# Projecting B with time on partitions, multiplying it by x four states at a time, and moving the clip and the last products to GpSimd

## The chip, the cores and the metric

The kernel runs on one core of a Trainium2 chip. The core has five engines that each work through their own list of instructions in order: TensorE (PE: matrix products; PEld is its weight load), VectorE (DVE), ScalarE (ACT), GpSimd (POOL) and SyncE (SP, which here only starts transfers). They wait for each other through semaphores alone. The metric is device time in microseconds; the median of several runs is compared.

## The reference

The input is 32 sequences ("batches") of 512 time steps and 256 channels. Each goes through three residual layers: a gated feed-forward layer, a state-space layer, and the first feed-forward layer again.

```python
def reference(x, ...):
    x = x + 0.5 * ffn(_layernorm(x), w_gate, w_up, w_down)
    x = x + ssm(_layernorm(x), W_in, b_in, W_dt1, b_dt1, W_dt2, b_dt2, A, D)
    x = x + 0.5 * ffn(_layernorm(x), w_gate, w_up, w_down)
    return x

def ffn(x, w_gate, w_up, w_down):          # 704 inner columns
    # fp4_linear: both operands are rounded to a grid of 8 magnitudes, in blocks of 16 with a
    # scale of max|x| / 6 each, and then multiplied
    h = silu(fp4_linear(x, w_gate)) * fp4_linear(x, w_up)
    return fp4_linear(h, w_down)

def ssm(x, W_in, b_in, W_dt1, b_dt1, W_dt2, b_dt2, A, D):   # 16 states, rank 64
    BC = x @ W_in + b_in
    Bm, Cm = BC[..., :16], BC[..., 16:]
    dt = clip(softplus((x @ W_dt1 + b_dt1) @ W_dt2 + b_dt2), 1e-07, 1e6)
    A_bar = exp(A * dt)
    B_barX = expm1(A * dt) / (A * dt) * dt * Bm * x
    # along time: h[t] = A_bar[t] * h[t-1] + B_barX[t], for each of 256 channels x 16 states
    return sum(h * Cm, axis=state) + D * x
```

## The kernel before

The weights are rounded to the grid once and stay in SBUF. Then each batch passes through `ffn 0`, `ssm` and `ffn 1`, and several batches are in work at a time.

**Order.** No loop decides which instruction stands where. Each operation is first recorded (`op`, L307 on) with its engine, a name and the tiles that it reads and writes. `Plan.run` then writes them out by a heap: of all operations whose inputs are written and whose buffers are free, the one with the smallest place comes next. The place is a number from the table `WHEN` (L31), by the operation's name and its count, plus `PERIOD` times the batch (L327). So every engine's list is fixed when the program is built, the same places hold for each batch, and the middle of the program repeats itself batch after batch. Lists are worked through strictly in order: an instruction that waits holds up everything behind it on its engine.

**The feed-forward layer.** `layernorm` (L507 to L522) takes statistics on DVE, four tiny operations on POOL, and writes the normalized rows on ACT. `quantize` rounds a tile to the grid: `top` (largest magnitude of each block, L544), `scale` (L546), `rinv` (L548) and `quotient` (L550) on DVE, `square` (L554) and `curve` (L556) on ACT, `grid` on PE (L563), `rounded` on ACT (L569) and `value`, times the scale, on POOL (L570). It works in the PSUM tile `q`, of which there is one, so roundings follow one another. A batch has four tiles of 128 time steps. Each tile takes `gate` and `up` (PE, L676) in two halves of 352 columns, `silu` (ACT, L686), the product of the two, a rounding of 704 columns, a turn (PE L710, ACT L715) and `down` (PE L722, L726, ACT L729). The product is made on POOL (`product`, L699), after ACT has copied `up` out of PSUM (`up copy`, L696). For the pair named in `BY_DVE`, tile 0 of `ffn 0`, DVE makes it from PSUM instead (`up silu`, L692, twice).

**The state-space layer.** Channels lie on partitions, in two halves `c` of 128, and time along the row. `bc` (L741) projects x to 32 rows, 16 of B and 16 of C. ACT adds their bias (L745), and one transfer puts them in DRAM as `rows` (L748). `dt1` (L741, bias L752) and `dt2` (L757) lead to `softplus` (ACT, L761, in PSUM) and to the clip `dt` on DVE (L764). Then, for each half and each two states (`NG` = 2):

- `load b` (L780) and `load c` (L782) fetch two rows of B and of C into all 128 partitions, 512 KB each;
- `exp` (L789) and `tanh` (L792) on ACT, of which the second writes one of two PSUM tiles `eb`;
- `x b` on POOL (L796): B times x, for both states in one instruction;
- `e` (L803), `e x b` (L806) and `scan` (L809) on DVE, for each state;
- `h c` on POOL (L812), and `sum states` on PE (L818).

In `x b` time is the outer and the state the inner loop. x is repeated over the two states; B's tile and the output are stepped through 512 numbers apart:

```python
bx().rearrange("p n l -> p l n"),
xT()[:, c, :].unsqueeze(2).to_broadcast([P, L, NG]),
bn().rearrange("p n l -> p l n"), ALU.mult),
```

All loads of B and C stand in SP's one list. Each waits until POOL has let go of the buffer that it fills; there are two buffers of each kind.

Of the kernel before, what the change touches and what calls it, by code (L numbers as in the profile page):

```python
# [16 lines left out]
P = 128  # L17
# [14 lines left out]
        "weights load": (7249, 7248, 7249, 7249, 6726, 6726, 6642, 6642, 6642, 6841, 6841, 6841,  # L32
        6841),
        "weights x top": (7249, 7065, 7353),
        "weights x scale": (7250, 7248, 7385),
        "weights x rinv": (7250, 7248, 7391),
        "weights x quotient": (7250, 7248, 7391),
        "weights x square": (7250, 7249, 7392),
        "weights x curve": (7250, 7249, 7392),
        "weights x grid": (7250, 7249, 7557),  # L40
        "weights x rounded": (7250, 7249, 7557),
        "weights x value": (7250, 7249, 7558),
        "weights turn": (7251, 7251, 7249, 7249, 7558, 7558),
        "weights turned": (7251, 7251, 7250, 7251, 7558, 7558),
        "weights load down": (7065, 6579),
        "weights h top": (7558, 6642),
        "weights h scale": (7571, 6642),
        "weights h rinv": (7571, 6642),
        "weights h quotient": (7571, 6643),
        "weights h square": (7590, 6643),  # L50
        "weights h curve": (7590, 6643),
        "weights h grid": (7590, 6643),
        "weights h rounded": (7590, 6643),
        "weights h value": (7795, 7065),
        "weights turn down": (7795, 7795, 7699, 7661),
        "weights turned down": (7897, 7814, 8179, 7699),
        "weights zero rows": (8077, 8345),
        "in load": (0,),
        "ffn 0 stats": (1267, 1773, 601, 2361),
        "ffn 0 mean": (1913, 2355, 1536, 3584),  # L60
        "ffn 0 var + eps": (4038,),
        "ffn 0 rstd": (4045,),
        "ffn 0 - mean": (3609,),
        "ffn 0 shift": (4249,),
        "ffn 0 normal": (4499, 5056, 6579, 4467),
        "ffn 0 x top": (6643,),
        "ffn 0 x scale": (6726,),
        "ffn 0 x rinv": (6822,),
        "ffn 0 x quotient": (6835,),
        "ffn 0 x square": (6841,),  # L70
        "ffn 0 x curve": (6873,),
        "ffn 0 x grid": (6880,),
        "ffn 0 x rounded": (6950,),
        "ffn 0 x value": (6969,),
        "ffn 0 xqT turn": (7065, 7129),
        "ffn 0 xqT turned": (7136, 7168),
        "ffn 0 tile 0 gate": (7353, 7251),
        "ffn 0 tile 0 silu": (7437, 7321),
        "ffn 0 tile 0 up": (7577, 7558),
        "ffn 0 tile 0 up silu": (7584, 7571),  # L80
        "ffn 0 tile 0 h top": (7590,),
        "ffn 0 tile 0 h scale": (7609,),
        "ffn 0 tile 0 h rinv": (7661,),
        "ffn 0 tile 0 h quotient": (7705,),
        "ffn 0 tile 0 h square": (7737,),
        "ffn 0 tile 0 h curve": (7808,),
        "ffn 0 tile 0 h grid": (7814,),
        "ffn 0 tile 0 h rounded": (7897,),
        "ffn 0 tile 0 h value": (8045,),
        "ffn 0 tile 0 turn h": (8301, 8192),  # L90
        "ffn 0 tile 0 turned h": (8352, 8339),
        "ffn 0 tile 0 down": (8397,),
        "ffn 0 tile 0 sum": (8461,),
        "ffn 0 tile 1 gate": (7385, 7392),
        "ffn 0 tile 1 silu": (7449, 7507),
        "ffn 0 tile 1 up": (7622, 7667),
        "ffn 0 tile 1 up copy": (7718, 7699),
        "ffn 0 tile 1 product": (7795,),
        "ffn 0 tile 1 h top": (7923,),
        "ffn 0 tile 1 h scale": (8000,),  # L100
        "ffn 0 tile 1 h rinv": (8032,),
        "ffn 0 tile 1 h quotient": (8121,),
        "ffn 0 tile 1 h square": (8179,),
        "ffn 0 tile 1 h curve": (8205,),
        "ffn 0 tile 1 h grid": (8217,),
        "ffn 0 tile 1 h rounded": (8275,),
        "ffn 0 tile 1 h value": (8416,),
        "ffn 0 tile 1 turn h": (8493, 8441),
        "ffn 0 tile 1 turned h": (8544, 8512),
        "ffn 0 tile 1 down": (8563,),  # L110
        "ffn 0 tile 1 sum": (8781,),
        "ffn 0 tile 2 gate": (8083, 8064),
        "ffn 0 tile 2 silu": (8096, 8070),
        "ffn 0 tile 2 up": (8134, 8345),
        "ffn 0 tile 2 up copy": (8256, 8390),
        "ffn 0 tile 2 product": (8429,),
        "ffn 0 tile 2 h top": (8576,),
        "ffn 0 tile 2 h scale": (8653,),
        "ffn 0 tile 2 h rinv": (8704,),
        "ffn 0 tile 2 h quotient": (8729,),  # L120
        "ffn 0 tile 2 h square": (8813,),
        "ffn 0 tile 2 h curve": (8838,),
        "ffn 0 tile 2 h grid": (8857,),
        "ffn 0 tile 2 h rounded": (8953,),
        "ffn 0 tile 2 h value": (8979,),
        "ffn 0 tile 2 turn h": (9088, 9081),
        "ffn 0 tile 2 turned h": (9165, 9126),
        "ffn 0 tile 2 down": (9222,),
        "ffn 0 tile 2 sum": (9267,),
        "ffn 0 tile 3 gate": (8077, 8109),  # L130
        "ffn 0 tile 3 silu": (8089, 8211),
        "ffn 0 tile 3 up": (8928, 8985),
        "ffn 0 tile 3 up copy": (9069, 9094),
        "ffn 0 tile 3 product": (9101,),
        "ffn 0 tile 3 h top": (9357,),
        "ffn 0 tile 3 h scale": (9376,),
        "ffn 0 tile 3 h rinv": (9440,),
        "ffn 0 tile 3 h quotient": (9472,),
        "ffn 0 tile 3 h square": (9510,),
        "ffn 0 tile 3 h curve": (9529,),  # L140
        "ffn 0 tile 3 h grid": (9587,),
        "ffn 0 tile 3 h rounded": (9613,),
        "ffn 0 tile 3 h value": (9677,),
        "ffn 0 tile 3 turn h": (9837, 9843),
        "ffn 0 tile 3 turned h": (9869, 9856),
        "ffn 0 tile 3 down": (9920,),
        "ffn 0 tile 3 sum": (9984,),
        "ssm stats": (8768, 8992, 9517, 10048),
        "ssm mean": (9325, 9369, 9933, 10093),
        "ssm var + eps": (10099,),  # L150
        "ssm rstd": (10150,),
        "ssm - mean": (10157,),
        "ssm shift": (10163,),
        "ssm normal": (10182, 10169, 10227, 10176),
        "ssm xT turn": (10233, 10246),
        "ssm xT turned": (10304, 10310),
        "ssm bc": (10425,),
        "ssm bc bias": (10489,),
        "ssm rows": (10656,),
        "ssm dt1": (10317,),  # L160
        "ssm dt1 bias": (10451,),
# [120 lines left out]
        "ffn 1 tile 3 sum": (18157,),  # L282
        "out store": (19712,),
}


class Buf:

# [598 lines left out]
```

## Time and profile before

| What | Value |
|---|---|
| Median of 3 runs | 3603.8 us (3603.49 to 3605.61) |
| The profiled execution's own time | 3604.13 us |
| Its span, first to last instruction | 3602.2 us |
| Mean granted TensorE clock | 0.984 |
| Busy over the span: DVE, ACT, PE, POOL | 3409.9, 3385.7, 3348.0, 3332.3 us |
| Results stored, first to last | 395.7 to 3598.4 us |
| Transfers moved | 578.36 MB, 161 GB/s |

All figures but the median are of one execution, taken by the hardware profiler. A line such as `L764` is line 764 of the kernel. A group of instructions is shown as `out<-in`, partitions x elements, and `xcount | busy us, mean ns of one | idle time of the engine just before them <-what ended it`. Instructions that follow each other on an engine overlap a little, so the mean duration times the count is more than the busy time. What an instruction takes of its engine's list is better read from the timeline, from one start to the next start.

### The profile page before, as it was taken

To read this page: it belongs to the slowest core of one execution; us is meant where nothing else is said; L and a number is where in the kernel's file an instruction comes from. 1 tells how busy PE (TensorE), PEld (TensorE's weight loads), DVE (VectorE), ACT (ScalarE), POOL (GpSimd) and SP (SyncE) were. 2 spreads that over 40 slices of the span, in tenths; PEclk is the share of its full clock that TensorE was granted. 3 is DMA by queue.
4 is the path that set the end of the run, shared out by engine and by line. 5 is a ranking of instruction groups with operands and counts; after the bars stand their busy time and mean duration, and the time that the engine had idled before them with its cause. 6 is when DMAs were issued, how large, how long until landed. Compare 5 with 4: busy or idle time off the path is not lost. (4 is left out here: it accounts for less than half of the span.)

```text
span 3602.2 us, 51333 instructions
## 1 busy us (share of the span) xinstructions
PE 3348.0 (93%) x16604; PEld 2443.6 (68%) x16826; DVE 3409.9 (95%) x5280; ACT 3385.7 (94%) x5813; POOL 3332.3 (93%) x1963
## 2 busy tenths in 40 slices
PE   5779999999999999999999999999999999999966
PEld 3457777667767767777766776776777776777654
DVE  3699999999999999999999999999999999999992
ACT  4689999999999999999999999999999999999973
POOL 2589999999999999999999999999999999999992
PEclk9899999999999999999999999999999999999988
DMA  1354545444545545454544454444555454445440
GB/s 45 112 173 166 173 164 176 165 169 165 176 171 170 165 158 175 170 173 164 177 165 169 165 176 170 170 165 159 176 171 173 163 177 165 168 161 169 171 170 12
DMA packets 186652, 578.36 MB, mean 161 GB/s; under 512 B 19664, under 2 KB 54032, under 8 KB 186384
## 3 DMA queue, kind: packets, MB, share of 16 engines
q1 hardware_dynamic: 184816, 574.89, 46.7%
q8 instruction: 133, 2.18, 0.2%
q14 instruction: 135, 1.11, 0.1%
q10 hardware_dynamic: 1568, 0.18, 0.0%
HBM read 556.12 MB, written 18.87 MB: 160 GB/s over the span
## 5 line engine op out<-in xcount | busy, mean ns | idle before, releaser
L676 PE MATMUL pt<-w_guT,xqT 128*128 128x352 f32 x4096 | 1317.4, 466 | 26.1 <-DVE dt L764 16.3
L812 POOL TENSOR_TENSOR hs<-hs,bc 128x1024 f32<-128x1024 f32 x512 | 1214.0, 2371 | 9.3 <-DVE hs L809 2.6
L809 DVE TENSOR_TENSOR_SCAN hs<-ab,eb 128x512 f32<-128x512 f32 x1024 | 1202.4, 1197 | 4.5
L796 POOL TENSOR_TENSOR bx<-xT,bc 128x1024 f32<-128x1024 f32 x512 | 1171.2, 2294 | 30.3 <-DVE eb L806 15.9
L676 PEld LDWEIGHTS pt<-w_guT,xqT 128*128 128x128 f32 x4096 | 753.3, 192 | 409.7 <-DVE dt L764 24.0
L792 ACT ACTIVATE eb<-dt,a_half 128x512 f32<-128x512 f32 x1024 | 708.1, 700 | 36.1 <-DVE hs L809 29.5
L806 DVE SCALAR_TENSOR_TENSOR eb<-eb,a_inv,bx 128x512 f32<-128x512 f32 x1024 | 734.9, 743 | 2.7
L722 PE MATMUL pt<-w_dT,hqT 128*128 128x256 f32 x3072 | 717.0, 383 | 14.8 <-ACT hqT L715 14.8
L789 ACT ACTIVATE ab<-dt,a_sb 128x512 f32<-128x512 f32 x1024 | 700.8, 727 | 1.5
L803 DVE SCALAR_TENSOR_TENSOR eb<-ab,eb 128x512 f32<-128x512 f32 x1024 | 684.5, 682 | 11.4 <-ACT eb L792 7.6
L722 PEld LDWEIGHTS pt<-w_dT,hqT 128*128 128x128 f32 x3072 | 580.1, 192 | 140.4 <-ACT hqT L715 32.9
L818 PE MATMUL py<-ident,hs 128*128 128x128 f32 x4096 | 536.1, 276 | 26.1 <-POOL hs L812 25.8
L818 PEld LDWEIGHTS py<-ident,hs 128*128 128x128 f32 x4096 | 469.4, 142 | 102.0 <-POOL hs L812 38.3
L570 POOL TENSOR_TENSOR h_q<-h_q,h_sc 128x704 f32<-128x704 f32 x258 | 360.3, 1397 | 53.2 <-ACT h_q L569 52.6
L699 POOL TENSOR_TENSOR h<-h,sl 128x704 f32<-128x704 f32 x224 | 379.0, 1692 | 27.4 <-ACT h L696 22.4
L544 DVE TENSOR_REDUCE q<-h 128x44 f32<-128x704 f32 x258 | 227.0, 880 | 68.6 <-POOL h L699 43.8
L710 PE MATMUL pt<-ident,h_q 128*128 128x128 f32 x1536 | 237.0, 278 | 41.2 <-ACT h L696 24.1
L563 PE MATMUL q<-h_m,eye 128*128 128x192 bf16 (+1 forms) x873 | 191.6, 305 | 70.9 <-ACT h_m L556 62.0
L710 PEld LDWEIGHTS pt<-ident,h_q 128*128 128x128 f32 x1536 | 180.5, 141 | 110.3 <-ACT h L696 51.8
L563 PEld LDWEIGHTS <-eye 128*128 128x128 bf16 x1300 | 125.2, 99 | 183.9 <-issue 106.8
L715 ACT COPY hqT<-pt 128x256 f32<-128x256 f32 (+1 forms) x512 | 233.9, 487 | 6.1 <-PE pt L710 5.7
L686 ACT ACTIVATE sl<-pt 128x352 f32<-128x352 f32 x512 | 222.5, 463 | 16.6 <-PE pt L676 13.8
(78 smaller groups left out, 4134.6 us busy)
## 6 DMA issues: line engine op xcount, KB each, us to landing
bc<-rows SPq DMA_DIRECT2D x1024, 512.0 KB, 4.1
x<-in_L_attn_x_dram SPq DMA_DIRECT2D x32, 512.0 KB, 5.2
out_dram<-x SPq DMA_DIRECT2D x32, 512.0 KB, 7.3
rows<-bc SPq DMA_DIRECT2D x32, 64.0 KB, 3.4
xn<-in_L_ffn_w_up_dram SPq DMA_DIRECT2D x6, 128.0 KB, 2.2
h<-in_L_ffn_w_down_dram SPq DMA_DIRECT2D x2, 352.0 KB, 3.4
xn<-in_L_ffn_w_gate_dram SPq DMA_DIRECT2D x5, 128.0 KB, 2.2
w_dt_sb<-in_L_attn_W_dt_dram ACTq DMA_DIRECT2D x2, 64.0 KB, 5.5
```

Source lines behind the costliest of these rows:

```text
L676: pe.matmul(to()[:, :HALF], lhsT=xqT()[:, c, j * P : (j + 1) * P], rhs=w_guT()[:, c, o : o + HALF], start=(c == 0), stop=(c == NC - 1),)
L699: op("POOL", "product", lambda sl=sl, h=h: g.tensor_tensor(h(), h(), sl(), ALU.mult), [h, sl], [h])
L710: pe.transpose(pt()[:, i * P : (i + 1) * P], hq()[:, kcol[k] : kcol[k] + P], ident)
L722: pe.matmul(po()[:, :DM], lhsT=hqT()[:, k, :], rhs=w_dT()[:, k, :], start=(k == 0), stop=False,)
L789: op("ACT", "exp", lambda c=c, i=i, k=k, ab=ab: s.activation(ab()[:, i, :], dt()[:, c, :], AF.Exp, scale=a_sb[:, c, k : k + 1]), [(dt, c)] ...
L792: op("ACT", "tanh", lambda c=c, i=i, k=k, eb=eb: s.activation(eb[i](), dt()[:, c, :], AF.Tanh, scale=a_half[:, c, k : k + 1]), [(dt, c)], ...
L796: op("POOL", "x b", lambda c=c, bx=bx, bn=bn: g.tensor_tensor(bx().rearrange("p n l -> p l n"), xT()[:, c, :].unsqueeze(2).to_broadcast([P ...
L803: op("DVE", "e", lambda i=i, ab=ab, eb=eb: v.scalar_tensor_tensor(eb[i](), ab()[:, i, :], 1.0, eb[i](), ALU.add, ALU.mult), [(ab, i), eb[i ...
L806: op("DVE", "e x b", lambda c=c, i=i, k=n + i, eb=eb, bx=bx: v.scalar_tensor_tensor(eb[i](), eb[i](), a_inv[:, c, k : k + 1], bx()[:, i, : ...
L809: op("DVE", "scan", lambda i=i, h=h, ab=ab, eb=eb: v.tensor_tensor_scan(h()[:, i, :], ab()[:, i, :], eb[i](), 0.0, ALU.mult, ALU.add), [(a ...
L812: op("POOL", "h c", lambda h=h, cn=cn: g.tensor_tensor(flat(h()), flat(h()), flat(cn()), ALU.mult), [h, cn], [h])
L818: pe.matmul(py()[:, j, :], lhsT=h()[:, i, j * P : (j + 1) * P], rhs=ident, is_transpose=True, start=False, stop=False, skip_group_check=True,)
```

## The change

- **B.** It is projected by itself, with time on partitions: for each 128 time steps, 16 columns and a product with a row of ones for the bias (`project b`). ACT copies the result out as `bT`, 128 x 64. Four transfers write it to DRAM as `rows_b`, where the four states of a group (`XG` = 4) lie side by side for each time step.
- **`load b`** fetches one group of four states, 1 MB, into all partitions. `x b` works on four states and half of the time steps, 128 x 256 x 4 = 1024 numbers per partition as before. B's tile is now read in the order in which it lies; x is repeated over four states; the output is still stepped through 512 numbers apart. There are as many `x b` as before.
- **C and dt.** C's 16 rows and `dt1`'s 64 rows come from one product of 80 rows (`project`, `project bias`).
- **The clip** `dt` moves from DVE to POOL; `softplus` now writes SBUF.
- **Products.** All tiles' products are made on POOL, with `up copy` on ACT.
- **Places.** New numbers for all operations; batches 0, 1, 30 and 31 have tables of their own, and the weights use batch 0's.

```diff
+FIRST = {
...
+PRODUCT_BY_DVE = set()
+VALUE_BY_DVE = set()
+CLIP_BY = "POOL"
...
-        o.at = (WHEN[o.name][k] + self.batch * PERIOD, len(self.ops))
+        table = self.tables.get(self.batch, WHEN)
+        o.at = (table[o.name][k] + self.batch * PERIOD, len(self.ops))
...
-    BY_DVE = {(0, 0)}
...
-    plan = Plan()
+    plan = Plan({0: FIRST, 1: SECOND, NB - 2: LAST_BUT_ONE, NB - 1: LAST})
...
-        op("PE", "bc", lambda: project(pbc()[: 2 * N, :], w_in_sb), [xT], [pbc])
-        bc = new(sp, [2 * N, L], F32, "bc", 1)
...
+        def project_b():
+            for j in range(NJ):
+                to = pb()[:, j * N : (j + 1) * N]
+                for c in range(NC):
+                    pe.matmul(to, lhsT=xT()[:, c, j * P : (j + 1) * P], rhs=w_b_sb[:, c, :],
+                              start=(c == 0), stop=False)
+                pe.matmul(to, lhsT=one_row, rhs=b_b_sb, start=False, stop=True)
+
+        op("PE", "project b", project_b, [xT], [pb])
+        bT = new(sp, [P, NJ, N], F32, "bT", 2)
+        op("ACT", "b turned", lambda: s.copy(flat(bT()), pb()[:, : NJ * N]), [pb], [bT])
+        rows_b = new(dr, [N // XG, L, XG], F32, "rows_b", 2)
...
+                for i in range(N // XG):
+                    nc.sync.dma_start(
+                        rows_b()[i].rearrange("(j p) n -> p j n", p=P),
+                        bT()[:, :, i * XG : (i + 1) * XG])
...
-            op("DVE", "dt", lambda c=c: v.tensor_scalar(
-                dt()[:, c, :], p2[c](), 1e-7, 1e6, ALU.max, ALU.min), [p2[c]], [(dt, c)])
...
+                op("POOL", "dt", lambda c=c: g.tensor_scalar(
+                    dt()[:, c, :], dt()[:, c, :], 1e6, 1e-7, ALU.min, ALU.max),
+                   [(dt, c)], [(dt, c)])
...
+                if n % XG == 0:
+                    bn = new(st, [P, L, XG], F32, "bn", 2)
+                    bx = new(st, [P, XG, L], F32, "bx", 2)
+                    op("SP", "load b", lambda n=n, bn=bn: nc.sync.dma_start(
+                        bn(), rows_b()[n // XG].partition_broadcast(P)), [rows_b], [bn])
+                    for o in range(0, L, L * NG // XG):
+                        t = slice(o, o + L * NG // XG)
+                        op("POOL", "x b", lambda c=c, bx=bx, bn=bn, t=t: g.tensor_tensor(
+                            bx()[:, :, t].rearrange("p n l -> p l n"),
+                            xT()[:, c, t].unsqueeze(2).to_broadcast([P, L * NG // XG, XG]),
+                            bn()[:, t, :], ALU.mult), [(xT, c), bn], [(bx, o)])
```

## The prediction

> **What bounds the kernel now.** I read the totals by engine first, then busy time by stretches of the span.
>
> ```profile
> PE 3348.0 (93%) x16604; PEld 2443.6 (68%) x16826; DVE 3409.9 (95%) x5280; ACT 3385.7 (94%) x5813; POOL 3332.3 (93%) x1963
> ```
> ```profile
> 0.00:135.60 135.60, 83.88 (x291) 50.46 (x294) 45.18 (x100) 67.36 (x106) 34.25 (x38) 0.92 0.18 56
> 1600.00:2000.00 400.00, 385.72 (x1940) 283.54 (x1967) 397.76 (x619) 395.02 (x680) 390.25 (x229) 1.00 0.50 170
> 3517.60:3602.20 84.60, 55.91 (x217) 38.91 (x217) 14.81 (x28) 30.82 (x55) 19.07 (x15) 0.84 0.04 13
> ```
> The columns after the length are PE, PEld, DVE, ACT and POOL busy. In the middle four engines are almost full: DVE 99.4%, ACT 98.8%, POOL 97.6%, PE 96.4%. DVE sets the pace, and no other engine is far behind it. Before the first scan (135.6 us) and after the last (3517.6 us) all stand idle most of the time.
>
> The timeline of the stores gives the beat: one batch per 1779.05 - 1672.60 = 106.4 us.
>
> ```profile
> 1672.60 0.43 SPq L849 DMA_DIRECT2D out_dram<-x  x1
> 1779.05 0.43 SPq L849 DMA_DIRECT2D out_dram<-x  x1
> ```
> So the execution's 3604.1 us (3602.2 of span and 1.9 around it, 0.3 above the median of the runs) is 32 x 106.4 = 3405 and 199 for both ends. Per batch DVE is busy 0.994 x 106.4 = 105.8 us, ACT about 105.0 (394.5 of 400 in most stretches), POOL 103.7 (389.9 of 400). The change touches the beat and the ends; I work out both.
>
> **The beat, on DVE.** The groups that are removed, kept or moved:
>
> ```profile
> L764 DVE TENSOR_SCALAR dt<-pt 128x512 f32<-128x512 f32 x64 | 40.4, 671 | 14.9 <-ACT pt L761 14.9
> L692 DVE TENSOR_TENSOR h<-pt,sl 128x352 f32<-128x352 f32 x64 | 32.8, 512 | 13.3 <-PE pt L676 10.2
> L796 POOL TENSOR_TENSOR bx<-xT,bc 128x1024 f32<-128x1024 f32 x512 | 1171.2, 2294 | 30.3 <-DVE eb L806 15.9 <-DMA bc<-rows 14.2
> L812 POOL TENSOR_TENSOR hs<-hs,bc 128x1024 f32<-128x1024 f32 x512 | 1214.0, 2371 | 9.3 <-DVE hs L809 2.6 <-DMA bc<-rows 1.5 <-PE pt L676 1.2
> L570 POOL TENSOR_TENSOR x_q<-x_q,x_sc 128x1024 f32<-128x1024 f32 x67 | 129.7, 1936 | 60.5 <-ACT x_q L569 60.5
> L699 POOL TENSOR_TENSOR h<-h,sl 128x704 f32<-128x704 f32 x224 | 379.0, 1692 | 27.4 <-ACT h L696 22.4 <-issue 2.7 <-DVE h_sc L546 1.6
> ```
> In the timeline two clips take 0.58 + 0.60 us of DVE's list, from start to start, and the two `up silu` 0.61 + 0.63. Per batch 2.4 us go.
>
> Something comes back, and only the new program's order shows it. In one batch of the repeating part, 17 DVE instructions read what the instruction just ahead wrote; before there were 4. New are 6 `e` to `e x b`, 3 `top` to `scale`, 3 `scale` to `rinv` and 2 `e x b` to `scan`; 1 went with `up silu`. The trace prices this:
>
> ```profile
> 1639.92 1.41 DVE L806 SCALAR_TENSOR_TENSOR eb<-eb,a_inv,bx 128x512 f32<-128x512 f32 x2
> 1641.24 1.21 DVE L809 TENSOR_TENSOR_SCAN hs<-ab,eb 128x512 f32<-128x512 f32 x1
> 1700.78 0.76 DVE L806 SCALAR_TENSOR_TENSOR eb<-eb,a_inv,bx 128x512 f32<-128x512 f32 x1
> 1701.64 1.22 DVE L809 TENSOR_TENSOR_SCAN hs<-ab,eb 128x512 f32<-128x512 f32 x1
> ```
> In the first pair of lines two `e x b` take 1.32 us, 0.66 each, and the scan reads the earlier one. In the second the scan reads the one right ahead and starts 0.86 us after it: 0.20 more. `scale` to `rinv` is 0.22 us when adjacent and 0.11 otherwise. No row has `e` to `e x b` or `top` to `scale` adjacent; 0.11 and 0.20 bound them, and I take 0.18, nearer the row with the same shape. 9 x 0.18 + 3 x 0.11 + 2 x 0.20 = 2.35, at least 1.7. So DVE changes by -0.7 to +0.1 us per batch; I take -0.2, a beat of 106.2.
>
> The Trainium skill, "VectorE: DVE Perf Modes", section "The DRAIN you can't avoid", says that a Vector instruction waits for an empty pipe in any case and that waits between chained ones cost nothing extra. The trace differs (0.86 against 0.66). By the page DVE would save the whole 2.4 us and ACT would set a beat of about 105.8.
>
> **The beat, on ACT.** Two more `up copy` at 0.33 us start to start, a 64-column copy at about 0.15 (256 columns take 0.26, 512 take 0.47), one bias less at 0.57, and 6 `square` to `curve` adjacent where 2 were, 0.15 each (0.79 against 0.64): 0.67 + 0.15 - 0.57 + 0.60 = +0.85. Table loads stay at 9 per batch. ACT comes to 105.8, just under DVE.
>
> **The beat, on POOL.** It gains a product (1.64 us start to start) and two clips. No row shows a one-input POOL operation of 512 numbers. Memsets give a lower bound: 204 ns for 128 columns and 98 for one, so 0.52 us for 512; the 16-fold `value` row scaled to 512 gives 1.06. I take 0.8, or 1.6 per batch. What `x b` costs now is the open price. Its old form (x repeated twice, B strided) takes 2.24 us from start to start; the flat product `h c` 2.33; `value`, whose scale is repeated 16 times, 1.89 for the same 1024 numbers. A repeated operand is cheaper, so a fourfold repeat and B in order should lie between 1.89 and 2.24; I take 2.05, and 2.33 as the upper end should the step of the output cost more. Without `x b` POOL is 103.7 - 16 x 2.24 + 1.64 + 1.6 = 71.1, with 2.05 it is 103.9; between the ends, with the clips' bounds, 100.8 to 108.9. Behind a clip that waits for `softplus` stand POOL's products and `h c`, hence DVE; the 2.3 us that POOL has free per batch cover that.
>
> The skill's "GPSIMD Engine Reference", section 4.1, speaks against the move as such: elementwise work belongs on VectorE, GpSimd being about twice as slow. The rows agree (704 numbers take 1692 ns as POOL's product and 879 as DVE's `quotient`), which matters only if POOL becomes the bound. Section 7 charges about one cycle per number for reading in steps over 8 bytes. The old `x b` reads B that way and is still quicker than the flat `h c`; by the rule the change would save 0.85 us on each `x b` (an estimate at that page's 1.2 GHz).
>
> PE loses a 512-column projection (4 rows of 0.6 us) and gains 12 matmuls of 16 columns (24 rows, at 0.11 us by the shortest weight load in the trace): about even, and 3.8 us are free per batch. Transfers: the four `rows b` write 2048 pieces of 16 bytes per batch. In the trace's packet records a 64-byte packet took 11 ns and a 4-byte one 9, so this adds some 20 us of packet time over 16 engines, 1.3 us per batch, to DMA engines half idle. If it were not hidden, it would come to 40 us in all. `load b` moves the same bytes in half as many transfers. On SP `load c` stands behind it as before; a load of 512 KB landed in 4.1 us, so 1 MB should in some 8, and each buffer now lasts two `x b`, about 13 us.
>
> **The ends.** At the start, roundings follow one another in the single `q`.
>
> ```profile
> 46.22 1.23 DVE L544 TENSOR_REDUCE pt<-xn 128x64 f32<-128x1024 f32 x1 [10.26 <-ACT w_guT L624]
> 62.72 0.90 DVE L544 TENSOR_REDUCE q<-h 128x44 f32<-128x704 f32 x1 [0.85 <-ACT h_q L569]
> 91.48 0.89 DVE L544 TENSOR_REDUCE q<-h 128x44 f32<-128x704 f32 x1 [5.87 <-POOL h L699]
> ```
> The third weight block waited 10.3 us, and tile 3's rounding began at 91.5, four after tile 0's with gaps of 6.6 to 13. In the new order the weight blocks run on, and tile 0, the second `down` block and tiles 1 to 3 follow directly, their gates and products ahead. With x quotients 6.4 apart (18.67, 25.04), the third at 34.7 as before, and five roundings 6.6 apart from about 47, tile 3's begins at 73: 18 us earlier. PE's gates and the new queue ahead of `exp` (two `x b` stand before the clips on POOL) may cost some of it: I take 14, between 0 and 20.
>
> At the tail the last scan is followed by one `ffn 1`:
>
> ```profile
> 3553.63 0.90 DVE L544 TENSOR_REDUCE q<-h 128x44 f32<-128x704 f32 x1 [20.82 <-POOL h L699]
> 3567.30 0.90 DVE L544 TENSOR_REDUCE q<-h 128x44 f32<-128x704 f32 x1 [11.14 <-POOL h L699]
> ```
> Tile 1's rounding waited 11.1 us because tile 1's `up` stood behind other tiles' gates. The new order puts it ahead. A rounding holds `q` 6.2 us (3553.6 to 3559.8), so tile 3's could begin at 3553.6 + 18.5 = 3572 instead of 3583.2: I take 10, between 0 and 12.
>
> **The sum.** 3604.1 - 30 x 0.2 - 14 - 10 = 3574.
>
> **Rivals.** (A) *The dependences hide.* If they fall where DVE would wait anyway, or cost 0.11, the beat goes to 105.4 (ACT's busy time counts some waiting, so it need not hold this). 30 x 1.0 + 26 gives 3548; with ends at their bounds and a beat of 105.0, 3530. For it: in the whole execution ACT idles 29.5 us waiting for scans, which could go too. Against: three engines would be over 99% full. (B) *POOL becomes the bound*, if `x b` does not get cheaper. It decides above (106.2 - 71.1) / 16 = 2.19 us per `x b`. Unchanged at 2.24 its beat is 106.9, 107.5 with the half per cent idle that DVE has now: 30 x 1.1 - 24 = +9, 3613. At 2.33 it is 108.4, or 109, and 3658. For it: the output keeps its step. Against: the 1.89 row. (C) *Cross waits.* Each engine fits, but three in fixed order at 98 to 99.8% wait for each other, and a beat of 107.0 to 107.3 eats the ends: 3600 to 3605. The trace's ACT and POOL show about 1.5 and 2.5% of such waiting behind a full DVE.
>
> **Chances.** The forecast 0.43, (A) 0.25, (B) 0.20, (C) 0.12. About 0.2% (7 us) is what a measurement of this kernel can tell from no change. The forecast and (A) are faster but for a few hundredths; (C) is mostly same; (B) is slower but for its mildest part. That makes 0.68 faster, 0.09 same, 0.23 slower. The range goes from 3525, just past (A)'s bound, to 3625, inside (B).
>
> **What would show it.** Right: stores about 106.2 us apart, `x b` near 2.05, clips under 1.06, `e x b` some 0.18 later behind its own `e`, the first scan near 120 us, 75 us from the last scan to the end. Wrong: POOL at 99% with `x b` at 2.2 or more; a beat over 106.4 with no engine over 99%; an unmoved first scan; or a beat under 105.5.

## The result, and the profile after

The changed kernel takes 3718.4 us (median of 3 runs, 3717.05 to 3725.01), against 3603.8 before: a ratio of 1.032, 95% interval 1.030 to 1.034. The prediction was 3574, range 3525 to 3625. Its sign was wrong, and the time lies outside its range.

The totals by engine, whole span (columns as before: busy us, share, instructions):

```profile
PE 3435.8 (92%) x17245; PEld 2561.3 (69%) x17466; DVE 3389.7 (91%) x5153; ACT 3415.7 (92%) x5879; POOL 3294.3 (89%) x2059
```

Busy time by stretches; the last one runs from the last scan to the end:

```profile
0.00:135.60 135.60, 94.36 (x333) 60.44 (x338) 50.84 (x104) 76.26 (x124) 42.94 (x44) 0.90 0.22 67
1600.00:2000.00 400.00, 380.77 (x1946) 284.67 (x1971) 379.68 (x577) 383.18 (x663) 370.11 (x232) 0.99 0.49 164
3637.00:3714.80 77.80, 58.17 (x235) 43.45 (x238) 14.80 (x28) 30.50 (x55) 18.36 (x15) 0.83 0.04 14
```

In the middle DVE fell from 397.8 to 379.7 us of 400, ACT from 395.0 to 383.2, POOL from 390.3 to 370.1. No engine is over 96%. DVE and POOL even have less work than before, by 20 and 38 us in the run. This is the picture that the prediction had listed under "wrong": a beat over 106.4 with no engine over 99%.

Two stores that follow each other, from the timeline of SP:

```profile
1490.02 0.42 SPq L1813 DMA_DIRECT2D out_dram<-x  x1
1599.69 0.42 SPq L1813 DMA_DIRECT2D out_dram<-x  x1
```

They are 109.7 us apart; before, 106.4. The spaces now differ from batch to batch, mostly 109.1 to 111; before, they agreed within 0.1 us until the end. The stores divide the span's extra 112.6 us so: the first store comes 19.1 us later, the next two spaces together are 16.9 shorter, the 25 spaces of the middle are 88.8 longer (3.55 each), and the last four 21.7 longer. The loss is the beat.

The groups that were priced, and two on ACT (mean ns of one, then the idle time ahead of them in the whole run and what ended it):

```profile
L1747 POOL TENSOR_TENSOR bx<-xT,bn 128x1024 f32<-128x1024 f32 x512 | 1037.8, 2039 | 31.8 <-DMA bn<-rows_b 26.3 <-DVE eb L1770 2.5 <-DVE eb L1767 2.0
L1776 POOL TENSOR_TENSOR hs<-hs,cn 128x1024 f32<-128x1024 f32 x512 | 1210.9, 2366 | 162.2 <-DMA cn<-rows_c 62.2 <-DVE mv L1438 15.7 <-PE pt L1698 15.3
L1718 POOL TENSOR_SCALAR dt<-dt 128x512 f32<-128x512 f32 x64 | 39.2, 612 | 35.2 <-ACT dt L1715 30.4 <-DVE hs L1773 1.3
L1703 ACT ACTIVATE bc<-pt,b_p_sb 80x512 f32<-80x512 f32 x32 | 21.9, 684 | 37.5 <-PE pt L1698 37.5
L1683 ACT COPY bT<-pt 128x64 f32<-128x64 f32 x32 | 6.8, 213 | 40.9 <-PE pt L1679 40.9
```

`x b` is cheaper, as hoped. What is new is the idle time: `h c` waited 9.3 us in the whole run before, now 162.2; ACT waits over 1 us per batch for each of the two projections. Folded over the batches between 1000 and 3000 us, most of the new waits lie in one stretch: POOL has 6.0 of its 7.3 us of waiting per batch in the 20 us behind `xT`, up to the first `x b` (before, 0.3 of 2.6), and DVE 4.0 of 5.1 in the 30 us behind it (0.4 of 0.6). In that stretch SP's list reads, in the timeline (start, time, transfer):

```profile
1539.88 2.02 SPq L1689 DMA_DIRECT2D rows_b<-bT  x4
1546.25 0.33 SPq L1743 DMA_DIRECT2D bn<-rows_b  x1
1546.68 0.38 SPq L1752 DMA_DIRECT2D cn<-rows_c  x1
```

and POOL's, later on:

```profile
1553.73 2.36 POOL L1776 TENSOR_TENSOR hs<-hs,cn 128x1024 f32<-128x1024 f32 x1 [2.66 <-DMA cn<-rows_c]
1556.19 4.03 POOL L1747 TENSOR_TENSOR bx<-xT,bn 128x1024 f32<-128x1024 f32 x2
```

`bT` is ready at 1539.9; four small transfers, one for each group of four states, write `rows_b`; the first `load b` waits till 1546.25 for its own to land; a `load c` of the old batch stands behind it and lands 6.9 us later; `h c` waits 2.7 us for that, and the new batch's first two `x b` start at 1556.2, 20 us after `xT` was copied. The order of the list itself costs time here: the load that stands first fetches the third group, and is issued 0.02 us after the third small transfer has landed, in each of the 18 batches between 1000 and 3000 us. The transfer of the first group, which the first `x b` needs, had landed at 1543.2, 3 us earlier.

One more thing shows in this stretch: the granted TensorE clock (the column after the five engines).

```profile
1536.00:1540.00 4.00, 4.00 (x28) 3.53 (x27) 3.93 (x8) 3.07 (x6) 4.00 (x3) 1.00 0.35 135
1540.00:1544.00 4.00, 4.00 (x13) 2.14 (x11) 3.97 (x7) 2.82 (x6) 1.77 (x2) 0.57 0.26 8
1544.00:1548.00 4.00, 3.95 (x17) 2.00 (x18) 2.58 (x6) 3.97 (x6) 3.48 (x2) 1.00 0.47 35
```

Of the 18 batches between 1000 and 3000 us it falls to a half in 11 right behind B's short products, for 3.41 us or twice that, and in three some 22.6 us behind `xT`. In the middle of the kernel before it never does.

So there were four suspects: (S) the transfers and their order on SP, (P) PE's time in the projections, with or without the clock, (O) the new order as such, and (W) the work that was moved to POOL.

### The profile page after: what moved, and what is told of

It reads as the page before. It is cut to its first block, busy times and chain, and to the rows that moved or that the text cites. A ratio compares the mean times of both kernels' runs of the same rounds, so it can differ in the third digit from the quotient of the medians.

```text
span 3714.8 us, 52128 instructions
## 1 busy us (share of the span) xinstructions
PE 3435.8 (92%) x17245; PEld 2561.3 (69%) x17466; DVE 3389.7 (91%) x5153; ACT 3415.7 (92%) x5879; POOL 3294.3 (89%) x2059
## 4 chain that ended last, share of the span: by engine, by line
PE 42%; ACT 18%; POOL 15%; DVE 11%; DMA 9%; issue 4%; SPq 1%; ACTq 0%; POOLq 0%; DVEq 0%
PE pt L1610 15%; PE pt L1656 10%; POOL hs L1776 6%; PE py L1782 6%; POOL bx L1747 5%; DMA cn<-rows_c 4%; ACT eb L1762 3%; PE q L1492 3%; DMA rows_b<-bT 3%; ACT ab L1759 3%; DVE hs L1773 3%; PE pt L1644 2%; DVE eb L1770 2%; PE pt L1677 2%; DMA bn<-rows_b 2%
## 5 line engine op out<-in xcount | busy, mean ns | idle before, releaser
L1776 POOL TENSOR_TENSOR hs<-hs,cn 128x1024 f32<-128x1024 f32 x512 | 1210.9, 2366 | 162.2 <-DMA cn<-rows_c 62.2
L1747 POOL TENSOR_TENSOR bx<-xT,bn 128x1024 f32<-128x1024 f32 x512 | 1037.8, 2039 | 31.8 <-DMA bn<-rows_b 26.3
L1770 DVE SCALAR_TENSOR_TENSOR eb<-eb,a_inv,bx 128x512 f32<-128x512 f32 x1024 | 745.0, 747 | 54.2 <-POOL bx L1747 42.3
L1759 ACT ACTIVATE ab<-dt,a_sb 128x512 f32<-128x512 f32 x1024 | 719.3, 732 | 1.6
L1782 PE MATMUL py<-ident,hs 128*128 128x128 f32 x4096 | 524.7, 277 | 22.4 <-POOL hs L1776 22.2
L1633 POOL TENSOR_TENSOR h<-h,sl 128x704 f32<-128x704 f32 x256 | 431.5, 1686 | 40.6 <-ACT h L1630 32.7
L1644 PE MATMUL pt<-ident,h_q 128*128 128x128 f32 x1536 | 250.9, 281 | 34.0 <-POOL h_q L1504 31.1
```

The lines of the kernel that those rows point to most:

```text
L1633: op("POOL", "product", lambda sl=sl, h=h: g.tensor_tensor(h(), h(), sl(), ALU.mult), [h, sl], [h])
L1644: pe.transpose(pt()[:, i * P : (i + 1) * P], hq()[:, kcol[k] : kcol[k] + P], ident)
L1747: op("POOL", "x b", lambda c=c, bx=bx, bn=bn, t=t: g.tensor_tensor(bx()[:, :, t].rearrange("p n l -> p l n"), xT()[:, c, t].unsqueeze(2).t ...
L1759: op("ACT", "exp", lambda c=c, i=i, k=k, ab=ab: s.activation(ab()[:, i, :], dt()[:, c, :], AF.Exp, scale=a_sb[:, c, k : k + 1]), [(dt, c)] ...
L1770: op("DVE", "e x b", lambda c=c, i=i, k=n + i, eb=eb, bx=bx: v.scalar_tensor_tensor(eb[i](), eb[i](), a_inv[:, c, k : k + 1], bx()[:, k % ...
L1776: op("POOL", "h c", lambda h=h, cn=cn: g.tensor_tensor(flat(h()), flat(h()), flat(cn()), ALU.mult), [h, cn], [h])
```

## The experiments

All times are medians, each beside runs of the kernel before on the same chip (3603 to 3607 us). "Old places" are the kernel before's table, for all batches.

### Moving work to POOL in the kernel before (W)

One part alone: the clip on POOL.

```diff
-                p2[c](), p2[c](), AF.Softplus, bias=b_dt2_sb[:, c : c + 1]),
-               p2[c:], [p2[c]])
-            op("DVE", "dt", lambda c=c: v.tensor_scalar(
-                dt()[:, c, :], p2[c](), 1e-7, 1e6, ALU.max, ALU.min), [p2[c]], [(dt, c)])
+                dt()[:, c, :], p2[c](), AF.Softplus, bias=b_dt2_sb[:, c : c + 1]),
+               p2[c:], [(dt, c)])
+            op("POOL", "dt", lambda c=c: g.tensor_scalar(
+                dt()[:, c, :], dt()[:, c, :], 1e6, 1e-7, ALU.min, ALU.max), [(dt, c)], [(dt, c)])
```

> The kernel before with one part of the change, the clip on POOL: two instructions per batch leave DVE (.58 and .60 us) and come to POOL (.61 each in the changed kernel), at the same places; softplus writes dt itself. DVE, busy 99.4 per cent, is what sets that kernel's beat. If DVE alone sets it, the beat falls by 0.5 to 1.2 us: 3565 to 3588. If POOL's queue has to wait for softplus there, and the order of three engines leaves no room (the theory that failed to get its due in the prediction), it is 3605 to 3680.

Measured: 3637.5 us, 1.0094 (1.0077 to 1.0110): 34 us slower, a beat of 107.5. In the middle:

```profile
1600.00:2000.00 400.00, 381.77 (x1915) 277.11 (x1939) 389.55 (x603) 390.69 (x673) 390.29 (x238) 1.00 0.50 167
```

POOL's share is 97.6%, the same as before the edit, while all others fell. POOL got 2 x 0.61 us of work and the beat rose by 1.1. So POOL at 97.6% had next to no room in that order: of the rest, more than half is one wait, that of the tiny `rstd` for DVE's `mv` (25.7 us between 1200 and 3200). DVE's saving of 1.2 us bought nothing.

The other part alone: the last product that DVE did, on POOL.

```diff
-BY_DVE = {(0, 0)}
+BY_DVE = set()
```

> The kernel before with another part alone, the last product that DVE did given to POOL: DVE loses two up silu (.61 and .63), ACT gets two copies (.45 each), POOL one product (1.64), at the place of the up silu. DVE alone: 3565 to 3590. Cross waits: over 3605, as POOL has 2.7 us free in a batch and the product stands in a row of four instructions that pass a tile on.

Measured: 3676.3 us, 1.0202 (1.0186 to 1.0217), a beat of 108.5: 2.1 us for 1.69 us of POOL. In the waits between 1200 and 3200 us (us in all, times, longest) DVE now stands 3.3 us each time for POOL's product, while POOL's share is 97.0%:

```profile
DVE q L546 <- POOL h L701: 63.5, 19, 3.7
```

The reverse in the changed kernel, where POOL has room:

```diff
-CLIP_BY = "POOL"
+CLIP_BY = "DVE"
```

> The changed kernel with the clip back on DVE (two per batch from PSUM, .58 us each in the kernel before), at the changed kernel's places. If the clip on POOL, which waits for softplus and holds POOL's queue (30 us in the run), is a cause: 3700 or less. If not: DVE, which has about 5 us idle in a batch, takes it in, and the time stays within 10 us of 3718, or rises by up to 30 where the clip keeps DVE waiting for softplus.

Measured: 3730.7 us, 1.0358 (1.0335 to 1.0380): 12 slower than the changed kernel. The clip on POOL is not what costs the changed kernel its time, though it does cost the kernel before. The product was not moved back in the changed kernel; `before_b` below has both on DVE, at the old places, and loses more.

### PE's room in the kernel before (P)

```diff
-op("PE", "bc", lambda: project(pbc()[: 2 * N, :], w_in_sb), [xT], [pbc])
+op("PE", "bc", lambda: [project(pbc()[: 2 * N, :], w_in_sb) for _ in range(2)], [xT], [pbc])
```

> A load test of the kernel before: the projection of B and C is done twice on PE (four matmul passes of .43 us more in a batch, the second writes the same numbers again), everything else as it was. The prediction held 2.7 us more PE work in a batch for hidden, in 3.8 us that PE has free. If that room is real, nothing moves: 3600 to 3608. If PE's row stands on the path through the projections (xT, projection, bias, softplus), up to 1.7 us per batch show: up to 3660.

Measured: 3643.2 us, 1.0111 (1.0096 to 1.0126): 40 us, 1.26 per batch for 1.72 us of PE. The two projections take 5.48 us in a row in place of 3.77. The waits between 1200 and 3200 us show how it passes on:

```profile
ACT bc L745 <- PE pt L741: 18.2, 18, 1.0
DVE eb L803 <- ACT eb L792: 13.3, 18, 0.7
```

ACT's next instruction in order is the bias that needs the projection; its `tanh` is late, so DVE's `e` is. The 3.8 us that PE had "free" did not lie there.

Less work in that place, the two projections of the kernel before done as one of 96 rows, which takes four passes from PE and a bias step from ACT:

> The kernel before with its two projections (dt, and B with C) in one of 96 rows: four passes of .43 us less on PE and one bias step of .68 us less on ACT in a batch; every other place as it was. Four passes more cost it 40 us. If the beat follows PE's work in this stretch both ways: 3570 to 3595. If DVE and POOL, whose work stays, hold the beat: 3595 to 3606. Slower, over 3610, if B and C come later than before by the new order (their bias step now stands where dt's stood, so they should not).

Measured: 3607.2 us, 1.0004 (0.9995 to 1.0013): nothing. There DVE (99.1% in the middle) and POOL (97.2%) hold the beat. So an engine's work there can cost without its removal being worth anything.

### The places (O), buffers, and the tables of the ends

The changed kernel's instructions on the old places:

```diff
+OLD["ssm project"] = OLD["ssm dt1"]
+OLD["ssm project b"] = OLD["ssm bc"]
+OLD["ssm load b"] = OLD["ssm load b"][::2]
...
+WHEN = FIRST = SECOND = LAST_BUT_ONE = LAST = OLD
```

> The changed kernel's instructions at the places of the kernel before, for all batches: project where dt1 stood, project b where bc stood, rows b and rows c where rows stood, every second load b, x b one place earlier (both halves of a group have to be there before its first e x b), the first tile's copy and product where its up silu stood. Theory O (the new places are to blame): the beat falls to 106.5 to 107.5 and the time to 3590 to 3640. Theories S and P (structure): the beat stays over 108.5, 3680 or more.

Measured: 4016.3 us, 1.1148 (1.1132 to 1.1165). The new structure doesn't fit the old places at all, so going back to them is no cure. That the new places are free of fault doesn't follow from it.

More buffers with no instruction moved:

```diff
-        self.args, self.kw = (pool, shape, dtype), dict(tag=tag, name=tag, bufs=bufs)
+        more = {"cn": 3, "hs": 4}.get(tag, bufs)
+        self.args, self.kw = (pool, shape, dtype), dict(tag=tag, name=tag, bufs=more)
```

> The changed kernel with a third buffer for C's loads and a fourth for the scans' results, every engine's order exactly as it was. If the loop from batch to batch closes through buffers (a load or a scan that waits for h c to free one): the beat falls by 1 us or more, under 3690. If it closes through the engines' orders alone: within 15 us of 3718.

Measured: 3712.3 us, 1.0303 (1.0288 to 1.0318), 6 under the changed kernel: the loop does not close through these two kinds of buffer. Those of B were not tried.

One table for all but the first batch (`SECOND = LAST_BUT_ONE = LAST = WHEN`):

> The changed kernel with the table of the batches in the middle for the second and the last two batches as well (the first keeps its own, which has the weights). In the changed kernel's profile the last four spaces between stores take 351.6 us, in the kernel before 329.8, and one of 120.4 stands where the table changes. If the tables at the end are worse than none: 3690 to 3710. If the end's loss is only the slower beat: 3718 to 3735.

Measured: 3805.3 us, 1.0560 (1.0544 to 1.0576). A miss: the tables of the ends are worth 87 us, 76 of them at the start (first store at 490 us, against 415).

### The transfers (S)

First a re-ordering of several transfers at once:

```diff
+WHEN["ssm load b"] = (10560, 11017, 11350) + WHEN["ssm load b"][3:]
+WHEN["ssm rows c"] = (10406,)
+WHEN["ssm load c"] = (11349, 11351) + WHEN["ssm load c"][2:]
```

> The changed kernel with another order of the transfers on SP's list alone: rows c right behind rows b, the old batch's last loads of C ahead of the new batch's first load b, and load b in the order in which x b uses it (in the changed kernel the third one stands first and holds one of two buffers). Theory S, SP's list (a load c that stands behind a load b that waits for rows_b to land keeps POOL's h c waiting, and this closes the loop from batch to batch): POOL's idle time ahead of h c falls from 162 us in the run to under 50, the beat from 109.9 to about 107.5, the time to about 3640. Theory P (PE: B's short products stand on the path and ACT waits for them) and theory O (the whole order is to blame): under 15 us gained, 3700 or more.

Measured: 4221.8 us, 1.1721 (1.1702 to 1.1741). It decides nothing, as POOL's `x b` and `h c` moved too when their loads did (PE then waits up to 13 us for an `h c`). A cleaner edit moves one transfer in the finished order and leaves every other engine's list alone:

```diff
+        for i, o in enumerate(done):
+            if o.name == "ssm load b" and done[i - 1].name == "ssm rows b":
+                k = next(k for k in range(i, len(done)) if done[k].name == "ssm load c")
+                if not any(q.name == "ssm rows c" for q in done[i:k]):
+                    done.insert(i, done.pop(k))
```

> The changed kernel with one transfer of each batch moved: the load of C that stands on SP's list right behind the new batch's first load b (which waits for rows_b to land) is put ahead of it; its buffer is free some 5 us earlier. Every other engine has exactly the changed kernel's order. Theory S, this wait closes the loop: the h c that waits 2.7 to 4 us for it in each batch starts at once, and the beat falls by 2 to 2.7 us, to about 107.5; 3635 to 3660. Theory P, the products of B on PE close it: the wait of h c goes, but under 0.5 us of beat with it, over 3700.

Measured: 3728.3 us, 1.0349 (1.0334 to 1.0365). Theory S, as I had put it, falls. The waits between 1200 and 3200 us tell why, first in the changed kernel, then here:

```profile
POOL hs L1776 <- DMA cn<-rows_c: 44.6, 16, 4.0
POOL bx L1747 <- DMA bn<-rows_b: 3.2, 4, 1.3
```
```profile
POOL bx L1752 <- DMA bn<-rows_b: 47.5, 20, 3.9
POOL hs L1781 <- DMA cn<-rows_c: 8.6, 8, 2.1
```

The wait went from `h c` to the `x b` behind it. Both hang on the same thing, when `rows_b` lands; I had taken away one of its two branches, and of the two `load c` that stand behind the first `load b` in the changed kernel this moves one.

### B's short products: clock, PE time, or the chain behind them

Four kernels change only how B is made, at the changed kernel's places. B's bias rows out:

```diff
-                              start=(c == 0), stop=False)
-                pe.matmul(to, lhsT=one_row, rhs=b_b_sb, start=False, stop=True)
+                              start=(c == 0), stop=(c == NC - 1))
```

> The changed kernel without the rows that add B's part of the bias b_in (one short product for each 128 steps, four in a batch), which leaves B without its bias. PE has some 1.6 us less per batch, in the stretch in which ACT waits for the projections. Theory P: ACT's waits for both projections (78 us in the run) fall by a half, the beat by about 1 us, the time to about 3685. Theory S: the chain to rows_b gets shorter by the same 1.6 us, so it can move by up to 1 us per batch too; theory O: within 10 us of 3718.

Measured: 3696.0 us, 1.0258 (1.0243 to 1.0273). The same with the `load c` moved:

> The last kernel, and B's bias rows left out as well (B without its bias; PE 1.6 us less in a batch). The bias rows alone brought 22 us. If the loop runs through PE's projections and then through the late load of C, one after the other, the two gains add up (S plus 22, about 3615 to 3640). If they are two loops beside each other, the sum exceeds the parts only if each hides the other.

Measured: 3697.1 us, 1.0259 (1.0244 to 1.0274): the two edits don't add up, since moving the load brings nothing.

Products of 128 columns in place of 16:

```diff
-pe.matmul(to, lhsT=xT()[:, c, ...], rhs=w_b_sb[:, c, :], ...)
+pe.matmul(to, lhsT=xT()[:, c, ...], rhs=w_b_wide[:, c, :], ...)
```

> The changed kernel with B's weights and bias repeated eight times, so that each of B's short products has 128 columns in place of 16 (as the products of skip, whose passes start 112 ns apart too, as those of 16 columns do); ACT copies 16 of each 128. If the 16 columns are what makes the clock fall: the half-speed stretch of 3.4 us per batch goes, and with it 0.5 to 0.9 us of beat (in the changed kernel's profile, batches without it take 109.1 to 109.6, with it 109.7 to 110.4): 3690 to 3705. If the stretch comes from PE's waits: it stays, 3715 to 3730.

Measured: 3726.2 us, 1.0325 (1.0310 to 1.0341). No batch has the half-speed stretch right behind the short products any more (five have one some 24 us behind `xT`), so the 16 columns had brought it on; but the time does not fall. The short products now take 4.19 us in a row (3.44 with 16 columns), the projection behind them 1.94 (2.89 in the median before, up to 3.70 at half speed). PE's sum is 0.2 us shorter, and `bT` 0.75 us later.

Four of the twelve products:

```diff
-for c in range(NC):
-    pe.matmul(to, lhsT=xT()[:, c, ...], ..., start=(c == 0), stop=False)
-pe.matmul(to, lhsT=one_row, rhs=b_b_sb, start=False, stop=True)
+pe.matmul(to, lhsT=xT()[:, 0, ...], ..., start=True, stop=True)
```

> The changed kernel with four of B's twelve products: the second half of the sum and the bias left out, so B is not whole. PE has some 2.6 us less in a batch than the changed kernel, nearly all that the change added. If PE's added work is the main cause, at about 0.6 us of beat per us of PE as in the run with the projection done twice: the beat falls by 1.5 us or more, 3665 or less. If the hand-offs of the new places are the cause whatever PE does: 3690 or more, as with the bias rows out (3696).

Measured: 3659.6 us, 1.0144 (1.0129 to 1.0159): half of the loss is back (B is not whole here). And B whole, but turned from one projection of 96 rows:

```diff
+pe.transpose(pb()[:, j * N : (j + 1) * N], bc()[R : R + N, j * P : (j + 1) * P], ...)
```

> The changed kernel with B whole and without its twelve short products: C, dt and B come out of one projection of 96 rows (four passes, as those of 80 rows), one bias step, and PE turns B's 16 rows into columns in four short instructions. All else as in the changed kernel, every place kept. PE's stretch for the projections falls from 6.4 us to about 2.5, but rows_b now also waits for the bias step. If PE's added work is the cause: 3640 to 3670, as with eight products left out (3660). If that run gained by something else: over 3695.

Measured: 3769.5 us, 1.0452 (1.0438 to 1.0466). A clear miss of theory P: PE's work in this stretch is 1.88 + 0.42 us, the least of all, and the kernel is the slowest. Here `bT` has to wait for the bias step as well and is ready 5.58 us after `xT`, in place of 3.89. The timeline shows where that goes:

```profile
1238.68 2.34 POOL L1767 TENSOR_TENSOR hs<-hs,cn 128x1024 f32<-128x1024 f32 x1 [4.73 <-DMA cn<-rows_c]
1241.21 0.60 ACT L1445 ACTIVATE xn<-x,shift,rstd 128x256 f32<-128x256 f32 x1 [3.53 <-POOL shift L1442]
1243.07 0.69 DVE L1758 SCALAR_TENSOR_TENSOR eb<-ab,eb 128x512 f32<-128x512 f32 x1 [3.30 <-ACT eb L1753]
1243.80 0.59 PE L1486 MATMUL q<-h_m,eye 128*128 128x512 bf16 x1 [4.62 <-ACT h_m L1479]
```

The late load holds `h c`; behind `h c` on POOL stands the four-number `shift` of the next `ffn`; ACT's `normal` needs it; behind that stand `tanh`, for DVE, and `square` and `curve`, for PE. One transfer stops four engines.

For each batch whose second `xT` copy ends between 1000 and 3000 us I took the time from there to the issue of its first `load b` (in all kernels of the table 0.02 us after the third small transfer has landed) and to the start of its first `x b`. The medians:

| kernel at the changed kernel's places | first `load b` after `xT`, us | first `x b` after `xT`, us | time, us |
|---|---|---|---|
| b_thin | 8.60 | 18.49 | 3659.6 |
| no_b_bias | 9.11 | 19.30 | 3696.0 |
| c_ahead_no_bias | 9.33 | 19.56 | 3697.1 |
| changed kernel | 10.05 | 20.27 | 3718.4 |
| more_buffers | 10.11 | 20.42 | 3712.3 |
| c_ahead | 10.35 | 20.76 | 3728.3 |
| b_wide | 10.36 | 20.33 | 3726.2 |
| b_from_rows | 11.71 | 21.91 | 3769.5 |

From first to last that is 109.9 us of time, 3.43 per batch, for 3.11 us of the first `load b` and 3.42 of the first `x b`: about 1.0 to 1.1 us of beat for each us. PE's work doesn't sort the rows so: b_from_rows has little, b_wide less than the changed kernel. Nor does the end of `dt2`, the other path out of the projections: 8.18 us behind `xT` in both b_thin and no_b_bias, 11.17 in the changed kernel, 10.65 in b_from_rows.

The clock sorts them no better. Between 1000 and 3000 us it is at half for 58 us in the changed kernel, 72 in no_b_bias, which is faster, and 17 in b_wide, which is not. But b_from_rows has the most, 137, so the clock is a rival for part of its loss. An estimate of that part comes from the next section: between `before_b` and `before_b_wide` half speed falls from 160 us to 20, 7.8 us per batch, and the beat by 0.6. The 4.3 us per batch that b_from_rows has over the changed kernel would then be worth 0.3 of its 1.6 us.

`clip_dve`, which also moves work to DVE, has 10.13, 20.09 and 3730.7 and lies off the line by some 20 us.

### The part with B on the old places

B's part alone there, `x b` with two states at a time, so that each `x b` has its old place:

```diff
+PRODUCT_BY_DVE = {(0, 0)}
...
-CLIP_BY = "POOL"
+CLIP_BY = "DVE"
...
+bn()[:, :, o : o + NG], ALU.mult), [(xT, c), bn], [(bx, o)])
```

> The third part alone on the places of the kernel before: B projected with time on partitions, four states side by side in memory, its loads of 1 MB, C and dt in one projection of 80 rows; clip and first product stay on DVE, and x b still takes two states at a time (its B now in pairs that lie together), so that it fits the old places one for one. If moving work to POOL is the whole loss, and this part is what gives POOL room: at or below 3604, with x b below its 2.24 us. If the projections on PE and the chain through two transfers cost: 3640 to 3720, and PE's half-speed stretches show once in a batch as in the changed kernel.

Measured: 3763.2 us, 1.0446 (1.0428 to 1.0463), beat 111.4, clock at half for 6.8 or 10.2 us of nearly each batch. With products of 128 columns:

> The part with B on the old places, with products of 128 columns in place of 16 and nothing else changed (before: 3763, beat 111.4 with 7 to 10 us of every batch at half speed). If the fallen clock is that part's loss: half of that time comes back, the beat is 107 to 108.5 and the time 3625 to 3670. If it is only a symptom of waits: over 3730.

Measured: 3744.4 us, 1.0379 (1.0361 to 1.0396): most of the half-speed time is gone and only 19 us come back. One `x b` of each batch waits for its load, 5.2 us on average; the beat is 4.4 over the kernel before's. The waits between 1200 and 3200 us:

```profile
POOL bx L2020 <- DMA bn<-rows_b: 99.4, 19, 7.4
```

The first `x b` begins 21.81 us behind `xT` in `before_b` and 21.31 here, and both times lie within 6 us of the table's line over the first `x b` (3766 and 3750 by it), though these two stand on other places. `old_places`, with 21.87 and 4016, does not; there the late `x b` is not all that is wrong. And with the clip on POOL too:

> The same and the clip on POOL, at the old places. In the kernel before that step cost 34 us, with POOL full; here x b takes 2.18 us in place of 2.24, 1 us less in a batch. If POOL's fill was the reason: it costs under 15 us, or gains, against before_b_wide. If it is the clip's wait for softplus on POOL's queue: 25 us or more again.

Measured: 3738.0 us, 1.0366 (1.0350 to 1.0381), no slower (first `x b` at 21.44 us, 16 us below the line). The step that cost 34 us with POOL full costs nothing where POOL waits anyway.

No kernel of these beats the one before; one projection of 96 rows equals it.

## Why the prediction was wrong, point by point

**The instructions' own prices were near.** From one start to the next `x b` takes 1.98 us (predicted 2.05), the clip 0.69 (0.8 between 0.52 and 1.06). Busy time per batch changed by -0.6 us on DVE (predicted -0.2), +0.9 on ACT (+0.85), and -1.2 on POOL (+0.2; sixteen `x b` at 0.07 less and two clips at 0.11 less make up 1.3 of the 1.4). `e` to an adjacent `e x b` that reads it now takes 0.73 us in the median, where pairs that don't depend on each other take 0.60: a price of 0.13, where 0.18 was taken. The Trainium skill, "VectorE: DVE Perf Modes", section "The DRAIN you can't avoid", measured no such price on a chain of copies; the trace after differs from it as the one before did.

**The step that failed is "the beat is the busiest engine's sum".** It gave -0.2; measured was +3.55 per batch in the middle. Rival (C) had the mechanism, engines in fixed order that wait for each other, but at 0.6 to 0.9 us and a chance of 0.12. What (C) lacked is the thing that they wait for. The prediction asked of the transfers how many bytes and how long each buffer lasts ("about 13 us") and found them hidden. It did not add up the latency from `xT` to the first `x b`. In the kernel before, for the batch whose `xT` was copied at 1594.5:

```profile
1600.54 0.42 SPq L748 DMA_DIRECT2D rows<-bc  x1
1604.54 2.15 SPq L780 DMA_DIRECT2D bc<-rows  x2
1609.96 2.29 POOL L796 TENSOR_TENSOR bx<-xT,bc 128x1024 f32<-128x1024 f32 x1
```

The first `load b` is issued 10.03 us behind `xT` in the median; in the changed kernel 10.05, so the loads start no later than they did. But what follows is longer: loads of 1 MB that land in 6.5 us in place of 512 KB in 4.1, the first of them for the third group, and two of the old batch's `load c` behind it. The prediction had `load c` "behind it as before"; before, all of the old batch's `load c` stood ahead of the first `load b`, in each of 19 batches. The first `x b` of a batch began 15.45 us behind `xT` before, now 20.27, and POOL's list is held up with it. The loop from batch to batch runs through this.

**PE "about even, hidden in 3.8 us"** was wrong twice. The stretch of the projections grew from 3.77 to 3.44 + 2.89 us. The passes that went were priced at their busy time, 0.6 us, but start 0.43 apart, so leaving four out saved 1.7 us and not 2.4. Of the new ones, the 16 short passes were priced right (1.86 us in a row without the bias rows), but the 8 of the bias rows take 1.6 and not 0.9. And the fallen clock adds 1 us to the projection behind. And PE's free time was not where it was needed: before_pe_twice.

**POOL's "2.3 us free per batch"**, named as the cover for a clip that waits, was no room in the old order: before_clip_pool. Rival (B)'s threshold for a full POOL (99%) was too high; in the kernel before it is 97.6.

**The ends** moved as worked out and by nearly as much: the first scan from 135.9 to 126.0 us (9.9, predicted 14), and the last scan's end is 77.9 us from the end of the span in place of 84.6 (6.7, predicted 10). Between first and last scan 129 us were lost. Some 40 of these lie outside the 25 middle spaces, above all where the tables change (one space of 120.4 us).

**Shown and not shown.** Shown: the cost is not the clip's place, C's buffers or those of the scans, the one `load c` alone, or the half speed behind the short products; and when only the making of B is changed, the time follows the moment when B lands in `rows_b`, by about 1.1 us for each us. Argued from the order of events, and not tried, is what the change itself made longer behind that moment: the larger loads, the third group first, the `load c` behind it. Open too: whether B's buffers matter; what holds b_thin at a beat of 108.2 us on average, 1.8 over the kernel before (its first `x b` still begins 3.0 us later); and whether an earlier `rows_b` (one transfer in place of four) or the load of the first group ahead of the third's, with all else kept, would bring the rest.

## What to carry to other kernels

When an engine's list is fixed, its idle few per cent are no reserve: price a step against the stretch where it lands, with who stands behind it in each list, and load that engine there by 1 us to see. For a value that comes round through memory, add up the whole path (product, copy, write, landing, load, the place in the queue) and set it against the time its first reader had; bytes per second and buffers don't show it. If taking one wait away only moves it to the next instruction, both wait for the same thing further up.

## What the runs showed of the hardware

- TensorE's clock fell to half for 3.41 us, or 6.83, with PE busy by its records in all of the 3.41 us ahead, right behind 24 passes of 16 columns, in 11 of 18 batches of the changed kernel (5 of 18 in clip_dve, which has the same products). With 128 columns per pass it never fell there. The Trainium skill, "TensorE: Matmul & The Clock Gate", section "What's actually happening", gives a free-running window of 3413 ns and the lower clock after an idle one; the length agrees, but here short products were enough, without an idle window by the records. Waits do it too: in three batches of the changed kernel it fell some 22.6 us behind `xT`, after 3.41 us in which PE was busy for 1.0 to 1.4; in b_from_rows it fell for 6.83 or 10.24 us in 16 stretches out of 18, most of them after 3.41 us with PE busy for 1.8 to 2.5.
- The price of that was small: in the middle of the changed kernel five of the six spaces between stores without it were 109.1 to 109.6 us, those with it mostly 109.7 to 110.4.
- A product of 1024 numbers on GpSimd took 2.04 us on average with x repeated four times and B in order, 2.18 repeated twice with B's pairs lying together (before_b), 2.29 before with B in 2048-byte steps, and 2.37 without repeats.
